# Exchanging kept exponentials through a DRAM buffer instead of by moves within SBUF, in a fused attention kernel

## The chip, the cores and the metric

One core of a Trainium2 chip runs the whole program. The metric is device time in microseconds (us): the median of several executions. The kernel was already tuned; it keeps TensorE, VectorE (DVE) and ScalarE (ACT) almost always at work, with GpSimd (POOL) and SyncE (SP) beside them for small sums and transfers.

## What is computed

`x` is 8 x 512 x 512 (batch, positions, features) in float32, with 16 heads of 32 features:

```python
Q = _split_heads(x @ Wq.T + bq);  K = _split_heads(x @ Wk.T + bk);  V = _split_heads(x @ Wv.T + bv)
cQ = Q + _split_heads(tokens @ Wq.T + bq)
cK = K + _split_heads(tokens @ Wk.T + bk)
scores = jnp.einsum('bhqd,bhkd->bhqk', cQ, cK) / jnp.sqrt(jnp.float32(HEAD_DIM))
attn = jax.nn.softmax(scores, axis=-1)
out = jnp.einsum('bhqk,bhkd->bhqd', attn, V)
# the result: x + out, heads joined again
```

## The kernel before

The work is cut into T = 32 steps: one step `t` is four heads of one of the eight batches. Steps 1 to 28 run in a software pipeline (`thirds`), each in three parts. In step t the kernel makes the row maxima of the scores of step t+1 (and begins those of t+2), the exponentials of t and t+1, the product of the exponentials with V for step t-1 (`weighted`), and a third of the projections of the next batch by seven-product block multiplication (`one_item`, `products`, `combine_x`).

The maxima need scores with queries on partitions; the product with V needs exponentials with keys on partitions. For half of the queries ScalarE computes the exponentials twice, once with queries on partitions for the sums and once with keys on partitions (L798). For the other half (query blocks 0 and 1 of the steps in `KEPT`, 1 to 29) it computes them once, with queries on partitions (`denominators`, L700), and **kept** in SBUF in `store`: `kept[t]` is 128 partitions x 4 blocks x 4 KB. They must then be transposed. VectorE does that within 32 x 32 blocks (`turn_kept`, L659), four instructions a step. What remains is to exchange blocks between the four groups of 32 partitions: block g of partition group a must trade places with block a of group g. There are six such pairs of 128 KB each.

Before, `swap_kept` makes this exchange with three DMAs for each pair: move 0 copies the one block aside (`between`, two spare slots of `store`), move 1 copies the other into its place, move 2 brings the first back from aside. Moves 0 and 1 for step t+1 stand at the end of step t, move 2 in the middle part of step t+1. SP issues some and POOL the others:

```python
later = 6 if t % 4 == 1 else 2
here = move == 2 or move == 0 and n >= later
(nc.gpsimd if here else nc.sync).dma_start(to, of)
```

`kept[t]` is read by TensorE in the next step, in the second half of the 32 products of `weighted` (`times_v_half`, L839).

The instructions of TensorE, ScalarE, VectorE and POOL stand in the order in which the program is written (`manual_schedule`); SP's are placed by a scheduler. Each engine works strictly in its own order and waits on semaphores.

POOL's other work in a step, in order: weighting and residual of the result (`send`, L912 and L913, which wait for VectorE's transpose L911), corrections to the projections (L538 to L540 for q, L532 for k, L1249, L1250 and L1238 for v), the split of the maxima into three bfloat16 parts (`split_max`, L714 to L717), the masked sums (`masked`, L864) and the bias (L203). In one step of four, sums of blocks of x are added (`combine_x`, L387 to L391). SP also issues the loads of x (`load_block`, L172), of the residual (`load_residual`, L190), the transposing DMA of the maxima (`turn_max`, L726) and the stores of the result (L916).

Of the kernel before, what the change touches and what calls it, by code (L numbers as in the profile page):

```python
# [9 lines left out]
F32 = mybir.dt.float32  # L10
# [7 lines left out]
def kernel(  # L18
# [38 lines left out]
    nc = tc.nc  # L57
    P = 128
    B, S, D = x.shape
# [3 lines left out]
    HG = P // HD  # L63
    NP = HG // 2
# [6 lines left out]
    KEPT = range(1, T - 2)  # L71
# [6 lines left out]
    op = ctx.enter_context(tc.tile_pool(name="op", bufs=2))  # L78
    ring = ctx.enter_context(tc.tile_pool(name="ring", bufs=1, space=bass.MemoryType.PSUM))

    psum = ring.tile([P, 8, 512], F32, tag="psum", name="psum")


# [47 lines left out]
    def begin(*ws):  # L131
        for w in ws:
            rows = order[w : w + 4]
            pairs = [(j, j + 1) for j in rows if j + 1 in rows]
            last = max(
                pairs, key=lambda p: rows.index(p[0]) + rows.index(p[1]), default=sorted(rows[2:])
            )
            order[w : w + 4] = [j for j in rows if j not in last] + list(last)
        row_of[0] = list(order)

    def released(*roles):
        order[:] = [row_of[0][i] for i in roles]
# [16 lines left out]
    BL = 32  # L159
    NB = S // BL  # L160

    def spread(a, d):

        return a.rearrange("(f j) d -> j f d", j=BL)[:, :, d : d + BL]

    def load_block(n):

        b, cc = divmod(n, NC)
        if b < B:
            xs[n] = xp.tile([P, NB, BL], F32, tag="x", name=f"x_{n}")  # L170
            for h in range(HG):
                nc.sync.dma_start(xs[n][h * BL : (h + 1) * BL], spread(x[b], cc * P + h * BL))  # L172
# [4 lines left out]
    def turned_by_vector(t):  # L177

        return t < T - 1

    def load_residual(t):

        b, g = divmod(t, G)
        if turned_by_vector(t):
            if t == T - 2:
                xr[t] = late[0][:, 2, :].rearrange("p (f e) -> p f e", e=BL)
            else:
                xr[t] = op.tile([P, NB, BL], F32, tag="xr", name=f"xr_{t}")
# [17 lines left out]
    store = EB.tile([P, 18, 2, S], F32, tag="eb", name="store")  # L206
# [20 lines left out]
    def load_w(n, w, queue, cs=range(NC)):  # L227
        wv = w.rearrange("(c p) d -> p c d", p=P)
        for c in cs:
# [7 lines left out]
                mybir.EngineType.Activation,  # L237
                mybir.EngineType.DVE,
                mybir.EngineType.Pool,
            }  # L240
        )
    )
# [133 lines left out]
    def load_blocks(most=B * NC):  # L376
        for _ in range(min(most, len(to_load))):
            load_block(to_load.pop(0))
# [185 lines left out]
    aside = const.tile([P, 2, 2, HS], F32, tag="aside", name="aside")  # L564
# [61 lines left out]
    def row_max_aside(t, qc):  # L626

        open_max(t)
        for j in range(HG):
            row_scores(t, qc, j, banks(j))  # L630
        nc.scalar.copy(spare, banks(0).rearrange("p (c f) -> p c f", f=P))  # L631
        for j in (1, 2, 3):
            one_max(t, qc, j, banks(j))

    def max_aside(t, qc):
        nc.vector.tensor_reduce(nmax[t][:, qc, 0:1, 0], spare, AX.XY, ALU.max, negate=True)
# [16 lines left out]
    kept = {}  # L653
# [4 lines left out]
        e = kept[t][:, :, n // NP, pr, :].rearrange("p g h s -> p g (h s)")  # L658
        nc.vector.transpose(e, e)  # L659

    APART = [(a, g) for a in range(HG) for g in range(a + 1, HG)]
    between = store[:, 16:18]

    def swap_kept(t, move, some=range(6)):

        later = 6 if t % 4 == 1 else 2

        def part(a, g):
            return kept[t][a * BL : (a + 1) * BL, g].rearrange("p c h s -> p (c h s)")

        for n in some:
            a, g = APART[n]
            at = (n + 2) % HG * BL
            aside = (store[:, 6:8] if t == KEPT[-1] else between)[at : at + BL, n // HG]
            aside = aside.rearrange("p i s -> p (i s)")
            to, of = [(aside, part(a, g)), (part(a, g), part(g, a)), (part(g, a), aside)][move]
            if t < KEPT[-1]:
                here = move == 2 or move == 0 and n >= later
            else:
                here = move > 0 and n >= 3  # L680
            (nc.gpsimd if here else nc.sync).dma_start(to, of)  # L681

    def denominators(t, qc, w=HG, js=range(HG)):

# [242 lines left out]
    part = {}  # L927
# [174 lines left out]
    turn_kept(1, 3)  # L1102
    combine_x(1, 1, nc.gpsimd)
    aparts[0] = masked(0)
    for move in range(2):
        swap_kept(1, move)

    MADE = [
        (n, u, product)
# [34 lines left out]
    def turn_more(t, i, after):  # L1144

        for _ in range((TURNED if t + 1 < KEPT[-1] else TURNED_LAST).get((i, after), 0)):
            if t + 1 in KEPT:
                n = turned[t + 1] = turned.get(t + 1, -1) + 1
                turn_kept(t + 1, n)
        even = t % 2 == 0  # L1150
        if (i, after) == ((2, 1) if even else (0, 2)) or (t, i, after) == (2, 0, 2):
            turn_x(next_x[0])
            next_x[0] += 1

    def thirds(t, made):

        b, r = divmod(t, G)
        of = (t - 1) // G + 1
        begin(0, HG)
        turn_more(t, 0, 0)  # L1160
        row_max_aside(t + 1, 1)
        max_aside(t + 1, 1)
        row_max(t + 1, 2, False, HG)
        turn_more(t, 0, 1)
        denominators(t + 1, 1, None, (1, 2, 3, 0))
        denominators(t + 1, 2, HG)
        weighted(t - 1, banks(0), banks(1), nothing)
        turn_more(t, 0, 2)
        load_blocks(1)
        one_item(of, *next(made), (2, 3), ignore, nothing)  # L1170
        released(0, 1, 4, 5, 7, 6, 2, 3)
        for i in (1, 2):
            begin(HG)
            rows = (t + 1, 3) if i == 1 else (t + 2, 0)
            if i == 1:
                joined(t, i - 1, rows)
                turn_more(t, i, 0)
                row_max(*rows, False, HG, False)
            else:
                exponentials_of_rest(t, i - 1)  # L1180
                turn_more(t, i, 0)
                row_max(*rows, False, HG)
            turn_more(t, i, 1)
            if i == 1:
                first = range(6 if t + 1 < KEPT[-1] else 3)
                swap_kept(t, 2, first)
                split_max(t + 1)
                turn_max(t + 1)
                swap_kept(t, 2, range(len(first), 6))
            dens = lambda js=range(HG): denominators(*rows, HG, js)  # L1190
            n, u, kind = next(made)
            if kind == "first":
                products(of, n, u, kind, False, dens, nothing, None)
                turn_more(t, i, 2)
            elif n == "v":
                small = nothing
                if t + 1 not in KEPT:
                    small = lambda: transpose_max(t + 1, banks(2), nc.scalar.copy)
                other_shared(of, n, u, dens, (0, 3), small, lambda: turn_more(t, i, 2))
                released(1, 2, 4, 5, 6, 7, 0, 3)  # L1200
            else:
                products(of, n, u, kind, False, dens, nothing, False)
                turn_more(t, i, 2)
            if i == 1:
                aparts[t] = masked(t)
            if (t + 1, i) == (KEPT[-1], 1):
                swap_kept(t + 1, 0)
            if i == 2:
                if r == 0:
                    combine_x(b + 1, 1, nc.gpsimd)  # L1210
                load_residual(t + 1)
            else:
                if t > 1:
                    bias_residual(t)
                if r == 0:
                    combine_x(b + 1, 0, nc.gpsimd)
            if i == 2 and t + 1 < KEPT[-1]:
                for move in range(2):
                    swap_kept(t + 1, move)

    def other_shared(b, n, u, dens, at, small, more):

# [44 lines left out]
    for t in KEPT[:-1]:  # L1267
        thirds(t, iter(MADE[(t - 1) % G * 3 :]))
# [56 lines left out]
    t = T - 3  # L1325
    begin(0, HG)
    first, second = row_of[0][:HG], row_of[0][HG:]
# [10 lines left out]
        row_max_of(t + 1, 2, 1, banks(HG + 2, 2))  # L1338
    row_max_of(t + 1, 2, 0, late[0][:, :2, :])
    bias_residual(t)  # L1340
    swap_kept(t, 1)
    apart = masked(t - 1)
    aparts[t] = masked(t)
    load_residual(t + 2)
    bias_residual(t + 2)
    swap_kept(t, 2)
    load_residual(t + 1)
    halves_of(t - 1, banks(0), (1,))
    row_of[0] = [*second[:2], *first[2:], *first]
# [22 lines left out]
    t = T - 2  # L1372
# [25 lines left out]
    t = T - 1  # L1398
# [48 lines left out]
    b, g = divmod(t, G)  # L1447
# [52 lines left out]
```

## Time and profile before

| | |
|---|---|
| median of 3 runs | 650.57 us (649.7 to 651.48) |
| the profiled execution | 650.74 us, span 648.9 us |
| granted TensorE clock | 1.0 throughout |
| busy share | PE 99%, DVE 93%, ACT 82%, POOL 63% |
| DMA | 102.01 MB, of them HBM read 19.75 MB and written 8.39 MB |
| exchange of kept exponentials | 264 DMAs on SP, 258 on POOL, 128 KB each |

PE is TensorE's matmuls, PEld its weight loads; q0 is the queue that POOL issues on, q1 SP's. A row of a timeline gives start, duration, engine, source line, operation, output and input, and in brackets the idle time before it with what ended it. L12 is line 12 of the kernel before; the changed kernel's lines stand one to four further down in most places.

### The profile page before, as it was taken

What the parts mean: (1) busy time and instruction counts of PE and PEld (TensorE: products, weight loads), DVE (VectorE), ACT (ScalarE), POOL (GpSimd) and SP (SyncE); (2) the same over time, 40 slices, a digit from 0 to 9 for tenths busy, and PEclk for the clock granted to TensorE, in tenths of its full rate; (3) what the DMA queues carried; (4) which work ended last, traced back from release to release, by engine and by line L of the source; (5) the groups of instructions that cost most, each with busy time, mean ns of one, the idle gap of its engine ahead of it and who ended that gap; (6) DMA issues with size and microseconds to landing.
All of it is one profiled execution on the core that took longest, in us unless ns stands there. A gap on an engine that the chain in (4) does not pass through costs nothing. (4 is left out here: it accounts for less than half of the span.)

```text
span 648.9 us, 24878 instructions
## 1 busy us (share of the span) xinstructions
PE 642.6 (99%) x9856; PEld 358.5 (55%) x9856; DVE 600.7 (93%) x845; ACT 533.6 (82%) x1364; POOL 409.6 (63%) x651
## 2 busy tenths in 40 slices
PE   9999999999999999999999999999999999999997
PEld 8445555556555555555555555555655555555541
DVE  3799999999999999999999999999999999999887
ACT  2479888889888889888888988898988888888564
POOL 3642555767666785668566585766767677675650
PEclk9999999999999999999999999999999999999999
DMA  7634588788779788878788887897877777777821
GB/s 187 106 48 68 121 183 175 158 180 178 155 172 181 156 190 181 190 155 172 173 184 172 171 170 152 177 198 158 180 152 180 176 162 153 165 177 161 201 37 33
DMA packets 248456, 102.01 MB, mean 157 GB/s; under 512 B 229962, under 2 KB 230474, under 8 KB 248340
## 3 DMA queue, kind: packets, MB, share of 16 engines
q1 hardware_dynamic: 234196, 65.54, 53.3%
q0 software_dynamic: 12384, 33.83, 19.2%
q8 instruction: 78, 1.28, 0.8%
q10 hardware_dynamic: 1760, 1.05, 0.6%
q14 instruction: 38, 0.31, 0.2%
HBM read 19.75 MB, written 8.39 MB: 43 GB/s over the span
## 5 line engine op out<-in xcount | busy, mean ns | idle before, releaser
L592 DVE TENSOR_REDUCE nmax<-psum 128x1 f32<-128x512 f32 x279 | 177.8, 676 | 9.9 <-PE psum L640 5.1
L681 POOL DMA_DIRECT2D store<-store x258 | 128.9, 502 | 77.3 <-DMA store<-store 51.9
L700 ACT ACTIVATE psum<-psum,nmax 128x512 f32<-128x512 f32 x248 | 165.1, 678 | 3.6 <-DVE nmax L592 3.0
L640 PE MATMUL psum<-kT,qT 32*128 32x512 f32 x1024 | 161.8, 612 | 0.0
L700 ACT ACTIVATE store<-psum,nmax 128x512 f32<-128x512 f32 x204 | 139.5, 700 | 24.7 <-DVE nmax L592 24.5
L798 ACT ACTIVATE store<-psum 128x512 f32<-128x512 f32 x232 | 119.8, 603 | 33.4 <-PE psum L784 33.4
L659 DVE STREAM_TRANSPOSE store<-store 128x1024 f32<-128x1024 f32 x116 | 138.9, 1217 | 0.0
L649 DVE TENSOR_REDUCE nmax<-psum 128x2 f32<-128x1024 f32 x98 | 118.9, 1213 | 0.0
L839 PE MATMUL psum<-store,v 128*32 128x256 f32 x1856 | 107.1, 381 | 0.6 <-issue 0.6
L839 PEld LDWEIGHTS psum<-store,v 128*32 128x32 f32 x1856 | 57.2, 110 | 57.9 <-ACT wT_q L631 21.2
L784 PE MATMUL psum<-qT,kT 32*128 32x256 f32 x928 | 83.8, 373 | 0.0
L640 PEld LDWEIGHTS psum<-kT,qT 32*128 32x128 f32 x1024 | 61.3, 183 | 35.5 <-issue 17.8
L912 POOL TENSOR_TENSOR res<-res,recs 128x512 f32<-128x512 f32 x30 | 31.4, 1045 | 75.4 <-DVE res L911 75.4
L784 PEld LDWEIGHTS psum<-qT,kT 32*128 32x128 f32 x928 | 60.8, 184 | 5.7 <-issue 0.3
L700 ACT ACTIVATION_READ_ACCUMULATOR psum<-psum,nmax 128x1 f32 x248 | 55.1, 222 | 0.0
L461 PE MATMUL psum<-wc_v,xc 128*32 128x256 f32 x768 | 47.7, 379 | 0.0
L203 POOL TENSOR_TENSOR xr<-xr,bvs 128x512 f32<-128x512 f32 x30 | 38.3, 1276 | 11.1 <-DMA x<-in_x_dram 11.1
L461 PE MATMUL psum<-xc,wc_q 128*32 128x256 f32 x720 | 44.8, 379 | 0.0
L461 PE MATMUL psum<-xc,wc_k 128*32 128x256 f32 x720 | 44.5, 379 | 0.0
L700 ACT ACTIVATION_READ_ACCUMULATOR store<-psum,nmax 128x1 f32 x204 | 44.4, 218 | 0.0
L913 POOL TENSOR_TENSOR res<-res,xr 128x512 f32<-128x512 f32 x30 | 38.3, 1276 | 2.4
L461 PE MATMUL psum<-xT,wT_k 128*32 128x256 f32 x480 | 34.5, 382 | 0.0
(191 smaller groups left out, 975.4 us busy)
## 6 DMA issues: line engine op xcount, KB each, us to landing
store<-store SPq DMA_DIRECT2D x264, 128.0 KB, 2.9
store<-store POOLq DMA_DIRECT2D x258, 128.0 KB, 3.8
out_dram<-res SPq DMA_DIRECT2D x122, 64.0 KB, 3.7
xr<-in_x_dram SPq DMA_DIRECT2D x120, 64.0 KB, 3.4
x<-in_x_dram SPq DMA_DIRECT2D x112, 64.0 KB, 3.5
w_q<-in_L_cond_Wq_dram SPq DMA_DIRECT2D x4, 256.0 KB, 4.5
w_v<-in_L_cond_Wv_dram SPq DMA_DIRECT2D x16, 64.0 KB, 2.5
w_k<-in_L_cond_Wk_dram SPq DMA_DIRECT2D x16, 48.0 KB, 2.8
```

Source lines behind the costliest of these rows:

```text
L203: nc.gpsimd.tensor_tensor(xr[t], xr[t], bias, ALU.add)
L461: nc.tensor.matmul(pt[r], still[:, r], moving, start=(kc == kcs[0]), stop=(kc == kcs[-1]))
L592: nc.vector.tensor_reduce(nmax[t][:, qc, j : j + 1, 0], pt, AX.X, ALU.max, negate=True)
L640: nc.tensor.matmul(pt, qkT["q", t][r, qc * P : (qc + 1) * P], qkT["k", t][r, :], start=True, stop=True,)
L649: nc.vector.tensor_reduce(nmax[t][:, qc, pr * 2 : pr * 2 + 2, 0], pt, AX.X, ALU.max, negate=True)
L659: nc.vector.transpose(e, e)
L681: (nc.gpsimd if here else nc.sync).dma_start(to, of)
L700: nc.scalar.activation(to, of, AF.Exp, bias=nmax[t][:, qc, j, :], accum_out=sums[t][:, qc, j, :],)
L784: nc.tensor.matmul(banks(j)[:, i * HS : (i + 1) * HS], qkT["k", t][r, kc * P : (kc + 1) * P], qkT["q", t][r, KQ * P :], start=False, stop= ...
L798: nc.scalar.activation(e[:, j], banks(j), AF.Exp)
L839: nc.tensor.matmul(pt[j * HD : (j + 1) * HD, half * HS : (half + 1) * HS], vs[b % 2][:, kc, (g * HG + j) * HD : (g * HG + j + 1) * HD], e, ...
L913: nc.gpsimd.tensor_tensor(y, y, xr.pop(t), ALU.add)
```

## The change

The exchange goes through a buffer in DRAM. `write_kept(t)` copies all twelve blocks that don't lie on the diagonal out of SBUF with six DMAs (one for each run of neighbouring blocks of a partition group); `read_kept(t)` brings them back, each to its new partition group, with six more. POOL issues all of them. The writes stand where moves 0 and 1 stood, the reads stand after the first third of the projections in the first part of the step, which is earlier than move 2 stood. SP's instructions are now in written order too, and the loads of x and of the residual are written behind the writes at the end of a step.

```diff
+    outside = ctx.enter_context(
+        tc.tile_pool(name="outside", bufs=2, space=bass.MemoryType.DRAM)
+    )
...
                 mybir.EngineType.Pool,
+                mybir.EngineType.SP,
...
-    APART = [(a, g) for a in range(HG) for g in range(a + 1, HG)]
-    between = store[:, 16:18]
-
-    def swap_kept(t, move, some=range(6)):
...
+    OTHERS = [(0, 1, 4), (1, 0, 1), (1, 2, 4), (2, 0, 2), (2, 3, 4), (3, 0, 3)]
+
+    def write_kept(t):
+
+        outer[t] = outside.tile([HG, BL, HG, NP * 2 * S // 2], F32, tag="kept", name=f"outer_{t}")
+        of = kept[t].rearrange("p g c h s -> p g (c h s)")
+        for a, lo, hi in OTHERS:
+            nc.gpsimd.dma_start(outer[t][a, :, lo:hi], of[a * BL : (a + 1) * BL, lo:hi])
+
+    def read_kept(t):
+
+        to = kept[t].rearrange("p g c h s -> p g (c h s)")
+        for g, lo, hi in OTHERS:
+            nc.gpsimd.dma_start(
+                to[g * BL : (g + 1) * BL, lo:hi],
+                outer[t][lo:hi, :, g].rearrange("a j f -> j a f"),
+            )
...
         turn_more(t, 0, 2)
-        load_blocks(1)
         one_item(of, *next(made), (2, 3), ignore, nothing)
         released(0, 1, 4, 5, 7, 6, 2, 3)
+        read_kept(t)
...
             if i == 1:
-                first = range(6 if t + 1 < KEPT[-1] else 3)
-                swap_kept(t, 2, first)
                 split_max(t + 1)
                 turn_max(t + 1)
-                swap_kept(t, 2, range(len(first), 6))
...
             if (t + 1, i) == (KEPT[-1], 1):
-                swap_kept(t + 1, 0)
+                write_kept(t + 1)
             if i == 2:
                 if r == 0:
                     combine_x(b + 1, 1, nc.gpsimd)
-                load_residual(t + 1)
+                if t + 1 == KEPT[-1]:
+                    load_blocks(1)
+                    load_residual(t + 1)
...
             if i == 2 and t + 1 < KEPT[-1]:
-                for move in range(2):
-                    swap_kept(t + 1, move)
+                write_kept(t + 1)
+                load_blocks()
+                load_residual(t + 1)
...
     bias_residual(t)
-    swap_kept(t, 1)
+    read_kept(t)
     apart = masked(t - 1)
     aparts[t] = masked(t)
     load_residual(t + 2)
     bias_residual(t + 2)
-    swap_kept(t, 2)
     load_residual(t + 1)
```

The order of TensorE, VectorE and ScalarE is the same line for line. The listing of POOL shows the change at two places. The first is the step after the blocks of x are combined, from the last sum of x (`xc`) over the result (`res`) and the corrections to q (`qT`). Before:

```order
L390 TENSOR_TENSOR xc<-xT 128x512
L391 TENSOR_TENSOR xc<-xT,xc 128x512
L912 TENSOR_TENSOR res_1937<-res_1937,recs_1935 128x512
L913 TENSOR_TENSOR res_1937<-res_1937,xr_1590 128x512
L538 TENSOR_TENSOR qT_1953<-qT_1953 128x256
L539 TENSOR_TENSOR qT_1953<-qT_1953 128x256
L540 TENSOR_TENSOR qT_1953<-qT_1953 128x256
L681 DMA store<-store 32x1024 x6
```

And now, where `outer` is the buffer in DRAM:

```order
L395 TENSOR_TENSOR xc<-xT,xc 128x512
L673 DMA outer_1840<-store 32x3072
L673 DMA outer_1840<-store 32x1024
L673 DMA outer_1840<-store 32x2048 x2
L673 DMA outer_1840<-store 32x1024
L673 DMA outer_1840<-store 32x3072
L913 TENSOR_TENSOR res_1919<-res_1919,recs_1917 128x512
L914 TENSOR_TENSOR res_1919<-res_1919,xr_1589 128x512
L542 TENSOR_TENSOR qT_1930<-qT_1930 128x256
L543 TENSOR_TENSOR qT_1930<-qT_1930 128x256
L544 TENSOR_TENSOR qT_1930<-qT_1930 128x256
```

Six writes now stand between the sum of x and the result; before, SP issued moves 0 and 1 of this step alone.

The second place is SP in the same and the next step: the transposed maxima (`maxT`), the residual (`xr`), the blocks of x, the moves and the results (`out_dram`). Before:

```order
L726 DMA_TRANSPOSE maxT_1746<-split 128x4x128
L190 DMA xr_1858<-in_x_dram 32x16x32
L172 DMA x_1948<-in_x_dram 32x16x32 x3
L681 DMA store<-store 32x1024 x12
L916 DMA out_dram<-res_1937 32x16x32 x4
L172 DMA x_1948<-in_x_dram 32x16x32
```

And now:

```order
L727 DMA_TRANSPOSE maxT_1728<-split 128x4x128
L175 DMA x_1847<-in_x_dram 32x16x32 x4
L193 DMA xr_1852<-in_x_dram 32x16x32 x4
L917 DMA out_dram<-res_1919 32x16x32 x4
L727 DMA_TRANSPOSE maxT_1998<-split 128x4x128
```

The moves are gone from SP, and the eight loads of a step stand together between the transposed maxima and the results.

More of the change, by code (lines that the diff above doesn't have):

```diff
@@ L659, in turn_kept @@
         nc.vector.transpose(e, e)
-    APART = [(a, g) for a in range(HG) for g in range(a + 1, HG)]
-    between = store[:, 16:18]
-    def swap_kept(t, move, some=range(6)):
[L666 to L681, printed above, removed]
+    outer = {}
+    OTHERS = [(0, 1, 4), (1, 0, 1), (1, 2, 4), (2, 0, 2), (2, 3, 4), (3, 0, 3)]
[11 more added lines that the diff above has]
+            )
     def denominators(t, qc, w=HG, js=range(HG)):
@@ L1104 @@
     aparts[0] = masked(0)
-    for move in range(2):
-        swap_kept(1, move)
+    write_kept(1)
     MADE = [
@@ L1217, in thirds @@
             if i == 2 and t + 1 < KEPT[-1]:
-                for move in range(2):
-                    swap_kept(t + 1, move)
+                write_kept(t + 1)
+                load_blocks()
+                load_residual(t + 1)
     def other_shared(b, n, u, dens, at, small, more):
```

## The prediction

> **What bounds the kernel now.** I read the page first, then the waits, then the timeline of each engine over four neighbouring steps. The page says who is busy:
>
> ```profile
> span 648.9 us, 24878 instructions
> PE 642.6 (99%) x9856; PEld 358.5 (55%) x9856; DVE 600.7 (93%) x845; ACT 533.6 (82%) x1364; POOL 409.6 (63%) x651
> q1 hardware_dynamic: 234196, 65.54, 53.3%
> q0 software_dynamic: 12384, 33.83, 19.2%
> ```
>
> TensorE, VectorE and ScalarE carry the span; GpSimd (POOL) is idle for a third of it, and the DMA queues are busy for some 73%. The list of waits says who waits for whom (total us, times, longest):
>
> ```profile
> POOL res L912 <- DVE res L911: 75.4, 27, 5.9
> POOL store L681 <- DMA store<-store: 51.9, 48, 3.2
> PEld psum L461 <- ACT store L798: 28.7, 50, 0.8
> PEld psum L839 <- ACT wT_q L631: 21.2, 28, 0.8
> DVE nmax L592 <- PE psum L640: 5.1, 11, 2.2
> PEld psum L461 <- POOL qT L538: 1.5, 4, 0.4
> PEld L771 <- DMA store<-store: 2.5, 6, 0.4
> ```
>
> TensorE waits for ScalarE, and VectorE for TensorE. The long waits on an exchange (L681) are POOL's own. Only 4 us of TensorE's waits are put down to POOL or a DMA, in pieces of at most 0.4 us. The query for the transpose that ends each step (L911) shows how regular this is:
>
> ```profile
> L911 DVE STREAM_TRANSPOSE res<-psum x28: 651/654/717, 73.6 to 591.5; 128x512 f32<-128x512 f32 x28
> ```
>
> 27 intervals in 517.9 us are 19.18 us a step. A step is therefore a ring of TensorE, ScalarE and VectorE, with POOL and the DMAs beside it. The listings of the two kernels show the same order on these three engines, line for line. So the change can gain nothing that these engines don't wait for today; it can only use up slack.
>
> **Part 1: POOL's time for the issues.** Per step 18 moves of 128 KB (9 of them on POOL on average) become 12 DMAs, all on POOL, and 24 blocks of 128 KB instead of 18. The only price in the trace is the move of 32 rows of 4 KB:
>
> ```profile
> L681 POOL DMA_DIRECT2D store<-store x258: 489/489/674, 78.9 to 613.8; - x129
> DMA to landing us min/median/max: 2.1/3.5/5.9
> ```
>
> A write names one run per partition (32 rows of 4, 8 or 12 KB), as the move does, so I take 0.49 us: 2.9 us for six. A read names one to three runs, 64 on average. If cost goes by the DMA it is 0.49 us, if it goes by the run 0.98 us, so six cost 2.9 to 5.9 us. I take 4.0, nearer to the lower end, since a part of the 0.49 must be fixed. The Trainium skill (DMA: Bandwidth & Descriptors, Anatomy of one DMA) says many descriptors can be emitted before their added cost shows; by that the six would cost 2.9. No run here shows it yet, as every move has the same 32 rows.
>
> What POOL has free in a step follows from two answers over four steps, first for L681 alone, then for all its work:
>
> ```profile
> sum 76.70, POOL 17.96; mean POOL 4.49
> sum 76.70, PE 76.70 PEld 43.55 DVE 73.77 ACT 67.21 POOL 52.92; mean PE 19.17 PEld 10.89 DVE 18.44 ACT 16.80 POOL 13.23
> ```
>
> Without the moves POOL works 34.96 us in 76.7. With 48 DMAs at 2.9 + 4.0 us a step it works 62.6; at 0.98 us each it would work 82.0, more than there is.
>
> **Part 2: POOL's order, where its results are needed.** The tightest place is the step after the blocks of x are combined (L391); there POOL runs without a gap. The timeline of POOL, then of VectorE:
>
> ```profile
> 294.79 0.27 POOL L714 CAST split<-nmax 128x16 bf16<-128x16 f32 x1
> ...
> 302.51 1.29 POOL L391 TENSOR_TENSOR xc<-xT,xc 128x512 f32<-128x512 f32 x1
> 304.06 1.05 POOL L912 TENSOR_TENSOR res<-res,recs 128x512 f32<-128x512 f32 x1 [0.26 <-DVE res L911]
> ...
> 307.24 0.73 POOL L539 TENSOR_TENSOR qT<-qT 128x256 f32<-128x256 f32 x1
> 307.92 0.74 POOL L540 TENSOR_TENSOR qT<-qT 128x256 f32<-128x256 f32 x1
> ...
> 318.02 2.00 POOL L681 DMA_DIRECT2D store<-store  x4 [0.20 <-issue]
> 323.24 1.04 POOL L912 TENSOR_TENSOR res<-res,recs 128x512 f32<-128x512 f32 x1 [3.22 <-DVE res L911]
> ...
> 326.40 0.73 POOL L1250 TENSOR_TENSOR v<-v 128x256 f32<-128x256 f32 x1
> ...
> 332.74 0.49 POOL L681 DMA_DIRECT2D store<-store  x1 [1.08 <-DMA store<-store]
> ```
> ```profile
> 309.42 0.42 DVE L554 TENSOR_TENSOR qT<-psum,qT 128x256 f32<-128x256 f32 x1 [0.24 <-ACT psum L700]
> 309.76 0.74 DVE L486 SCALAR_TENSOR_TENSOR qT<-psum,tok,qT 128x512 f32<-128x512 f32 x1
> ```
>
> Now POOL issues nothing between L391 and L912 (SP makes the moves there); afterwards the six writes stand between them (the listing with the diff). So 2.9 us of issuing move ahead of sums that VectorE needs. What comes before them moves too: the reads of the step before start when L1250 is done. That is 327.13 in the step of the same kind, so 38.4 us (two steps) sooner 288.7; with 0.5 us of waiting (part 3) and 4.0 of issuing they end at 293.2, where now L714 starts at 294.79. The 9.01 us of work up to the end of L391 (303.80) then end at 302.2, the writes at 305.1, and 3.91 us later (304.06 to 307.97) L539 at 309.0. VectorE uses that at 309.76: 0.8 us of slack are left, the wait is nil. With reads at 0.98 us it is 310.9 (1.1 us late), with all twelve so 313.9 (4.1 us). The place comes six times. In the other steps the 3.22 us before L912 cover the added 0.9 us of writes.
>
> **Part 3: data in time.** Every read waits for all six writes, so POOL stands still at the first one, and behind it stand the split of the maxima and the sums for L390. Then TensorE's second half of `weighted` waits for all six reads. The writes may start at 318.02 as L681 does now and are issued by 321.0. 12 blocks are 1.57 MB; q0 moved 33.83 MB in 19.2% of 648.9 us, 271 GB/s, so 5.8 us: 324.3 if they flow from 318.5. From the end of the flow to the semaphore I add 3.3 us (3.8 from issue to landing less 0.5):
>
> ```profile
> store<-store POOLq DMA_DIRECT2D x258, 128.0 KB, 3.8
> store<-store SPq DMA_DIRECT2D x264, 128.0 KB, 2.9
> out_dram<-res SPq DMA_DIRECT2D x122, 64.0 KB, 3.7
> xr<-in_x_dram SPq DMA_DIRECT2D x120, 64.0 KB, 3.4
> x<-in_x_dram SPq DMA_DIRECT2D x112, 64.0 KB, 3.5
> ```
>
> 327.6: POOL, free at 327.13, waits 0.5 us. The reads are issued by 331.6 (now the last move is at 332.74), their data flow until 333.9 and have landed at 337.2.
>
> ```profile
> 336.85 3.18 PEld L839 LDWEIGHTS psum<-store,v 128*32 128x32 f32 x64 [0.76 <-ACT wT_q L631]
> ```
>
> The second half begins at 338.4, so 1.2 us are left. The bounds: loads of x and of the residual share the engines (SP will issue eight in a row, behind the transposed maxima). q1's 53.3% are 346 us; less SP's 264 moves at q0's rate (128 us) they leave 218 us for 354 transfers of 64 KB, the weights and the transposed maxima, by estimate 0.5 us for a load, so eight could add 4 us. Then the writes land at 331.6, the reads at 341.2, 2.8 us late. Below, with no queueing, the slack is 2 us or more.
>
> SP loses its nine moves and its order is now fixed: outputs, transposed maxima, x, residual. x and the residual are loaded a step ahead of use, and the maxima are used in the next step; so I cost it at nothing, and the cover is most of a step of 19.18 us. The start keeps its order on the three engines: nothing. At the end the last exchange has less room:
>
> ```profile
> 599.00 2.36 DVE L659 STREAM_TRANSPOSE store<-store 128x1024 f32<-128x1024 f32 x2
> ```
> ```profile
> 619.06 1.45 PEld L839 LDWEIGHTS psum<-store,v 128*32 128x32 f32 x32 [0.76 <-ACT store L1318]
> ```
>
> Its writes can start at 601.4; by the same durations (0.5 + 5.8 + 3.3 for them, 9.6 for the reads) they have landed at 611.0 and the reads at 620.6, 1.5 us after TensorE wants them. With little else on the queues there it may be nothing; I take 0.5.
>
> **The sum.** The profiled run took 650.74 us for a span of 648.9 (1.84 us around it); the median of three is 650.57. Steps 0, start 0, end 0.5: 651.2.
>
> **The rivals.** (a) POOL's sums come late after L391: 1.1 to 4.1 us six times, 7 to 25 us, 658 to 676. It decides once a read costs over 0.8 us. For it: POOL has no gap there now. Against: the slack above. (b) The reads land late and TensorE waits for a DMA in each of 28 steps: 0.5 to 2.8 us, 14 to 78 us, 665 to 729, likelier in the lower half. It decides once write and read together take 1.2 us longer than in part 3. For it: the DMA engines now go from 18 to 24 blocks, and DRAM writes land later for their size (64 KB in 3.7 us against 128 KB in 2.9). The Trainium skill (the same section) says the semaphore waits for the write's receipt and that HBM's is the heaviest; the trace agrees in its sign, with 0.8 us. Against: today three moves in a row fit into the same stretch. (c) POOL becomes the bound at 82.0 us in four steps: 5.3/4 us, 28 times, 37 us, 688. (d) Faster: fewer bytes cross SBUF per exchange (24 block accesses for 36), and VectorE's transposes of `store` or ScalarE's exponentials shorten; 0.1 us a step would be 2.8 us, 648. Nothing in the waits speaks for it.
>
> **How the numbers follow.** No change 0.37, (a) 0.17, (b) 0.28, (c) 0.10, (d) 0.08. A change of 0.3% (2 us) is about what a measurement of this kernel can tell. Slower is (a) + (b) + (c), 0.55; same 0.37; faster 0.08. The forecast's own range is 649.5 to 652.5; the range reaches from (d)'s 648.5 to 690, leaving out the upper part of (b), some 0.15, and a little below.
>
> **What would show it.** Right: L911's successor 19.18 us apart, POOL waiting under 2 us at the first read, no wait of TensorE or VectorE for POOL or a DMA over 1 us. (a) shows as waits of L558/L490 for POOL every fourth step, (b) as TensorE at L840 waiting for a DMA in each step, (c) as POOL busy over 95%, (d) as shorter instructions. A read above 0.8 us or writes that need over 10 us to land make the forecast wrong.

## The result and the profile after

The changed kernel takes 693.34 us (median), the kernel before, on the same chip, 651.03 us: a ratio of 1.064, 95% interval 1.0601 to 1.0679. One of its four runs was in a slower state (702.44 us, at a granted clock of 0.975), as was one of the four with two queues below (694.89 us); the medians count them, the ratios leave them out. The profiled execution took 694.2 us for a span of 692.4 us. It is slower, by 43.5 us of span, and 3 us beyond the upper end of the range. The page:

```profile
span 692.4 us, 24189 instructions
PE 652.0 (94%) x9856; PEld 365.0 (53%) x9856; DVE 605.0 (87%) x845; ACT 536.6 (77%) x1364; POOL 461.2 (67%) x741
q0 software_dynamic: 22272, 91.25, 52.3%
q1 hardware_dynamic: 221524, 30.92, 36.4%
```

TensorE runs the same 9856 matmuls as before and stands still for 6% of the span; they take 652.0 us for 642.6, and its clock is halved in four stretches before its last matmul (last section). The waits of the same kernel say what it stands still for. In the lines of the changed kernel L840 is the product with V (L839 before), L673 the writes, L679 the reads, L206 the bias on the residual (L203 before):

```profile
PEld psum L840 <- issue: 41.1, 43, 6.8
PE psum L840 <- DMA store<-outer: 27.6, 15, 6.0
POOL store L679 <- DMA outer<-store: 16.9, 12, 2.5
POOL xr L206 <- DMA xr<-in_x_dram: 11.6, 4, 6.8
```

The first two rows are one wait, seen at the weight loads and at the matmuls: the second half of `weighted` waits for the reads. No wait of VectorE for POOL is in the list. The transpose that ends each step, L912 now, gives the length of a step, and the line of the reads what an issue costs:

```profile
L912 DVE STREAM_TRANSPOSE res<-psum x28: 652/655/718, 73.5 to 621.0; 128x512 f32<-128x512 f32 x28
```
```profile
L679 POOL DMA_DIRECT2D store<-outer x174: 502/534/619, 78.9 to 648.2; - x174
```

(621.0 - 73.5)/27 is 20.28 us a step, for 19.18. So the 43.5 us lie in three places: 29.6 us in 27 steps; 9.2 us in the two intervals behind them, up to the last result transposes (27.82 and 11.61 us for 26.41 and 3.82); and 4.9 us behind the last of these (32.0 us for 27.2). The start is as long as before.

What a long step looks like, on POOL first, where the blocks of x are combined (L391 to L395):

```profile
300.05 3.20 POOL L679 DMA_DIRECT2D store<-outer  x6 [0.83 <-DMA outer<-store]
...
309.89 1.28 POOL L394 TENSOR_TENSOR xc<-xT 128x512 f32<-128x512 f32 x1
311.12 1.28 POOL L395 TENSOR_TENSOR xc<-xT,xc 128x512 f32<-128x512 f32 x1
312.35 2.98 POOL L673 DMA_DIRECT2D outer<-store  x6
...
322.35 2.68 POOL L679 DMA_DIRECT2D store<-outer  x5 [2.40 <-DMA outer<-store]
```

and then on TensorE's weight loads, two steps of the same kernel:

```profile
309.63 1.45 PEld L840 LDWEIGHTS psum<-store,v 128*32 128x32 f32 x32 [0.76 <-ACT wT_q L635]
311.24 1.57 PEld L840 LDWEIGHTS psum<-store,v 128*32 128x32 f32 x32 [0.15 <-issue]
...
328.80 1.45 PEld L840 LDWEIGHTS psum<-store,v 128*32 128x32 f32 x32 [0.76 <-ACT wT_q L635]
332.79 1.48 PEld L840 LDWEIGHTS psum<-store,v 128*32 128x32 f32 x32 [2.54 <-issue]
```

In the first of the two steps the halves follow each other, as before. In the second the first half ends at 330.25, and the other half begins 2.54 us later: the last read lands at 332.47. From the first write (312.35) to the first read is 10.0 us, from there to the end of the wait (332.79) 10.44 us, in all 20.4 us. The writes had been held behind L394 and L395.

### The profile page after: what moved, and what is told of

Its sections match the earlier page's. It is cut to its first block, busy times and chain, and to the rows that moved or that the text cites. A ratio compares the mean times of both kernels' runs of the same rounds, so it can differ in the third digit from the quotient of the medians.

```text
span 692.4 us, 24189 instructions
## 1 busy us (share of the span) xinstructions
PE 652.0 (94%) x9856; PEld 365.0 (53%) x9856; DVE 605.0 (87%) x845; ACT 536.6 (77%) x1364; POOL 461.2 (67%) x741
## 3 DMA queue, kind: packets, MB, share of 16 engines
q0 software_dynamic: 22272, 91.25, 52.3%
q1 hardware_dynamic: 221524, 30.92, 36.4%
## 4 chain that ended last, share of the span: by engine, by line
PE 38%; DMA 29%; POOL 18%; DVE 5%; issue 5%; ACT 1%; SPq 1%; POOLq 0%; DVEq 0%
PE psum L465 19%; DMA store<-outer 14%; DMA outer<-store 11%; POOL store L679 5%; PE psum L644 5%; PE psum L840 5%; POOL outer L673 4%; PE psum L785 3%; PE psum L408 2%; DMA xr<-in_x_dram 2%; POOL v L1238 2%; DMA out_dram<-res 1%; POOL res L914 1%; PE psum L772 1%; POOL res L913 1%
## 5 line engine op out<-in xcount | busy, mean ns | idle before, releaser
L840 PE MATMUL psum<-store,v 128*32 128x256 f32 x1856 | 115.9, 396 | 27.8 <-DMA store<-outer 27.6
L679 POOL DMA_DIRECT2D store<-outer x174 | 93.0, 541 | 23.5 <-DMA outer<-store 16.9
L840 PEld LDWEIGHTS psum<-store,v 128*32 128x32 f32 x1856 | 60.4, 113 | 90.1 <-issue 41.1
L673 POOL DMA_DIRECT2D outer<-store x174 | 86.7, 505 | 8.9 <-DVE store L663 6.5
L206 POOL TENSOR_TENSOR xr<-xr,bvs 128x512 f32<-128x512 f32 x30 | 38.4, 1280 | 24.8 <-DMA x<-in_x_dram 13.2
```

The source lines that it names most:

```text
L673: nc.gpsimd.dma_start(outer[t][a, :, lo:hi], of[a * BL : (a + 1) * BL, lo:hi])
L679: nc.gpsimd.dma_start(to[g * BL : (g + 1) * BL, lo:hi], outer[t][lo:hi, :, g].rearrange("a j f -> j a f"),)
L840: nc.tensor.matmul(pt[j * HD : (j + 1) * HD, half * HS : (half + 1) * HS], vs[b % 2][:, kc, (g * HG + j) * HD : (g * HG + j + 1) * HD], e, ...
```

## The experiments

A step here is the mean over 27 intervals of the transpose, the end the two intervals behind them, the rest what follows up to the end of the span, all from the trace of each kernel. Ratios are to the kernel before in the same session (649.88 to 651.03 us), with their 95% intervals.

| kernel | us | ratio | step | end | rest |
|---|---|---|---|---|---|
| before | 650.57 | 1 | 19.18 | 26.4, 3.8 | 27.2 |
| changed | 693.34 | 1.064 (1.0601 to 1.0679) | 20.28 | 27.8, 11.6 | 32.0 |
| half rows | 654.05 | 1.0066 (1.0042 to 1.0090) | 19.14 | 26.4, 3.8 | 31.9 |
| three quarters | 656.06 | 1.0079 (1.0048 to 1.0110) | 19.18 | 27.6, 4.0 | 32.0 |
| wide writes | 679.93 | 1.0455 (1.0393 to 1.0518) | 19.93 | 27.9, 11.6 | 28.1 |
| long runs | 689.01 | 1.0614 (1.0576 to 1.0653) | 20.04 | 26.9, 10.3 | 32.0 |
| last exchange half | 686.86 | 1.0548 (1.0499 to 1.0597) | 20.18 | 28.9, 3.8 | 32.0 |
| early half | 676.78 | 1.0404 (1.0345 to 1.0462) | 20.03 | 27.9, 10.7 | 27.2 |
| two queues | 689.76 | 1.0589 (1.0530 to 1.0647) | 20.58 | 27.4, 6.2 | 28.0 |
| half rows in SBUF | 661.12 | 1.0172 (1.0149 to 1.0195) | 19.49 | 26.4, 5.1 | 28.7 |
| half rows, more DMAs | 649.99 | 0.9999 (0.9984 to 1.0014) | 19.17 | 26.4, 3.8 | 27.1 |
| old moves, SP written | 664.11 | 1.0214 (1.0183 to 1.0244) | 19.67 | 27.5, 5.4 | 27.1 |
| exchange only | 747.02 | 1.1456 (1.1411 to 1.1501) | 22.40 | 35.4, 3.8 | 31.9 |
| writes first | 677.22 | 1.0393 (1.0354 to 1.0432) | 19.64 | 27.8, 11.5 | 33.2 |
| all three | 667.60 | 1.0252 (1.0224 to 1.0280) | 19.57 | 33.5, 3.9 | 27.6 |

### Is it the data of the exchange? Half of each row, and three quarters

```diff
-  nc.gpsimd.dma_start(outer[t][a, :, lo:hi], of[a * BL : (a + 1) * BL, lo:hi])
+  nc.gpsimd.dma_start(outer[t][a, :, lo:hi, :512], of[a * BL : (a + 1) * BL, lo:hi, :512])
```

The reads likewise; with 768 for 512 it is three quarters. All twelve issues, their places and waits stay.

> Only the first half (2 KB) of every exchanged row is written and read back; the other half stays where it was, so the data of half a block is not exchanged. The twelve DMAs, their order and their waits are as in the changed kernel. Theory T (the DMA engines are full: 24 blocks of 128 KB and the small loads take more engine time than a step has room for) expects 650 to 656 us, since half the bytes are gone. Theory L (a fixed chain of write, receipt, wait on GpSimd, read is too long, whatever the bytes) expects 675 us or more. Theory S (the new written order of SyncE, with eight loads in one burst, is what delays things) expects 680 us or more.

> The changed kernel, but only the first 3 KB of each exchanged row of 4 KB are moved. Theory T (there is a deadline some 20 us after the first write, and only what lands behind it costs): the reads end 17 to 18 us after the first write, no step is longer than 19.3 us, 652 to 658 us, as with half the bytes. Rival C (each byte slows the engines or the queues, without a deadline): halfway between half and whole, steps of 19.6 to 19.8 us, 670 to 676 us.

Both came out as theory T has it: with half rows every step is as before, with three quarters every step but one (19.90 us; the kernel before has one of 19.85). The transposes with half rows, and the weight loads with three quarters, which follow each other in the step that was 2.54 us late:

```profile
L912 DVE STREAM_TRANSPOSE res<-psum x28: 650/653/657, 73.1 to 590.0; 128x512 f32<-128x512 f32 x28
```
```profile
336.66 3.18 PEld L840 LDWEIGHTS psum<-store,v 128*32 128x32 f32 x64 [0.76 <-ACT wT_q L635]
```

So there is a deadline, and bytes that land ahead of it cost nothing: neither POOL's added issues nor the traffic as such lengthens a step. From the records of the single packets, medians over the steps, in us from the first write's issue:

| of each row | write's data end | first read | reads' data take | reads' data end |
|---|---|---|---|---|
| 2 KB | 5.92 | 9.75 | 5.59 | 15.30 |
| 3 KB | 7.65 | 9.75 | 7.55 | 17.25 |
| 4 KB | 8.98 | 10.01 | 10.12 | 20.16 |

The second 0.79 MB costs the write 3.06 us (257 GB/s) and the reads 4.53 us (174 GB/s). With whole rows 20.16 us is longer than a step of the ring: 17 of 28 times the next writes are issued before the reads' data have ended, with half rows once. The time of half rows fell only to 1.0066 all the same: the last stretch stays 4.9 us longer (below).

### Is it the place of the writes on POOL?

```diff
             if i == 2:
+                if t + 1 < KEPT[-1]:
+                    write_kept(t + 1)
                 if r == 0:
                     combine_x(b + 1, 1, nc.gpsimd)
...
             if i == 2 and t + 1 < KEPT[-1]:
-                write_kept(t + 1)
                 load_blocks()
```

> The changed kernel with one move in GpSimd's order: in the step in which the blocks of x are combined, the six writes stand ahead of the second half of that combination (2.5 us of POOL's work) instead of behind it. Theory T (the deadline of the reads is missed by 2 to 3 us in that step because its writes are issued later than in the others): its writes start 2.5 us sooner in the step, its second half of weighted stops waiting, and these steps (20.6 to 24.1 us) fall to 19.9 to 20.4 us: 12 to 18 us less in all, 674 to 682 us. Rival (the long steps come from the combination and the sums behind it, not from the data): the steps stay, 690 to 695 us.

677.22 us, 16 us less: theory T again. The longest step is 20.40 us for 24.07. POOL, and TensorE's weight loads, in the step of the same kind as the one above:

```profile
305.65 2.99 POOL L673 DMA_DIRECT2D outer<-store  x6
308.66 1.29 POOL L394 TENSOR_TENSOR xc<-xT 128x512 f32<-128x512 f32 x1
...
315.94 3.20 POOL L679 DMA_DIRECT2D store<-outer  x6 [0.21 <-issue]
```
```profile
324.50 1.45 PEld L840 LDWEIGHTS psum<-store,v 128*32 128x32 f32 x32 [0.76 <-ACT wT_q L635]
326.89 1.48 PEld L840 LDWEIGHTS psum<-store,v 128*32 128x32 f32 x32 [0.94 <-issue]
```

The wait is 0.94 us for 2.54. So of the 29.6 us in the steps, 17 come from the writes held behind 2.5 us of sums in one step of four. The other 12.5 are smaller misses of the same deadline, in steps of every kind: with the writes first TensorE's second half still waits 0.5 to 2.2 us in 15 of 27 steps, mostly in every second one.

### Which part of the flow is slow?

> The six writes of 32 partitions become four writes of all 128 partitions, 4 KB runs, which also copy the diagonal blocks: 2.10 MB instead of 1.57 MB a step. The reads stay six of 32 partitions. If T holds because only 32 partitions are read at a time (the write phase took 8.4 to 9.4 us for 1.57 MB), the writes should end 2 us or more sooner in spite of their bytes, and the time falls to 655 to 680 us. If T holds by bytes alone, a third more to write makes it 700 to 715 us. L expects 685 to 700 us, two issues fewer and no other difference.

> The changed kernel, but the loads of x and of the residual and the stores of the results of batches 0 to 6 move 32 rows of 2 KB in place of 512 runs of 128 bytes: same bytes, same DMAs, the data lands in another arrangement, so the result is not the reference's. T expects most of the 36% of engine time of the SyncE queue to go and the time to fall to 652 to 670 us. L expects 688 to 695 us. S expects a part of the loss to go, 670 to 690 us.

Long runs is this edit, for the loads of x, of the residual, and the stores but those of the last batch:

```diff
-  nc.sync.dma_start(xs[n][h * BL : (h + 1) * BL], spread(x[b], cc * P + h * BL))
+  nc.sync.dma_start(
+      xs[n][h * BL : (h + 1) * BL].rearrange("p f e -> p (f e)"),
+      x[b][cc * P + h * BL : cc * P + (h + 1) * BL, :],
+  )
```

Wide writes: four DMAs of 128 partitions, the diagonal blocks with them, for six of 32.

```diff
-  for a, lo, hi in OTHERS:
-      nc.gpsimd.dma_start(outer[t][a, :, lo:hi], of[a * BL : (a + 1) * BL, lo:hi])
+  for g in range(HG):
+      nc.gpsimd.dma_start(outer[t][g].rearrange("a j f -> (a j) f"), of[:, g])
```

They move a third more bytes in the same time (2.10 MB, data end at 8.88 us; 236 GB/s over the phase for 175), and the reads' data end at 19.43 us for 20.16. The time lies at the end of the first expected range, but not for its reason, since the writes end no sooner; 4 of the 13 us saved are in the last stretch (28.1 us for 32.0, below). Long runs: the loads of x and the residual and most stores of results move 2 KB runs for 128 byte runs (the numbers in them are then not the kernel's). q1's share of the DMA engines fell from 36.4% to 25.2%, the exchange's data ended hardly sooner (8.82 and 19.43 us), and the kernel is barely faster. The loads' small packets are not what makes the exchange late.

> The changed kernel, but half of the six writes and half of the six reads (those of the partition groups 2 and 3) are issued by SP, in its written order ahead of the loads. All bytes move. Theory P (what limits a write or read is that one queue works on 32 partitions at a time: four wide writes moved 2.10 MB in the time of 1.57 MB): two groups are under way at once, the writes' data take 5 to 7 us instead of 9 and the reads' too, steps of 19.2 us, 652 to 660 us with the end shorter as well. Theory M (the rate of DRAM or of the DMA engines limits): 9 us each as before, steps of 20 us and more, 685 us and above. POOL then has 174 DMAs instead of 348.

```diff
-  nc.gpsimd.dma_start(outer[t][a, :, lo:hi], of[a * BL : (a + 1) * BL, lo:hi])
+  queue = nc.gpsimd if a < 2 else nc.sync
+  queue.dma_start(outer[t][a, :, lo:hi], of[a * BL : (a + 1) * BL, lo:hi])
```

The reads likewise. 689.76 us, against theory P. SP's reads are mostly issued 1 to 8 us behind POOL's, because SP has the eight loads and the stores in front of them, so the run is no clean test of the time. But where packets of both queues flow at once (297 to 302 us), their sum is 207 to 308 KB in a us by the records of packets, and one queue alone reaches 289 (POOL's, at 338 us) and 374 (SP's, at 317). The residual comes late as well:

```profile
POOL xr L206 <- DMA xr<-in_x_dram: 47.0, 12, 5.8
PE psum L842 <- DMA store<-outer: 25.3, 11, 4.3
```

> The changed kernel with the exchange split by time: whole blocks of 128 partitions are written (four writes for six, a third more bytes), the first 2 KB of each row two thirds into the step, as soon as they are turned, the second 2 KB at its end. All bytes move. Theory T: at the end of the step only half of the write's data stand ahead of the reads, so these end 15 to 17 us after that write instead of 19.7, before the deadline: steps of 19.2 to 19.4 us; the end stays long (27.8 and 11.6 us), 662 to 670 us. Rival D (the DMA engines as a whole are full, not the place of the data): steps of 19.9 us or more, 680 us and above. Rival P (the two more issues a step make POOL late): steps of four kinds, every fourth one over 21 us, 675 us and above.

```diff
-  if (t + 1, i) == (KEPT[-1], 1):
-      write_kept(t + 1)
+  if i == 1 and t + 1 <= KEPT[-1]:
+      write_kept(t + 1, (0,) if t + 1 < KEPT[-1] else (0, 1))
...
-  write_kept(t + 1)
+  write_kept(t + 1, (1,))
```

Here the second argument names the halves of each row that are written, as four wide writes each. 676.78 us: by its steps of 20.03 us rival D, though 3 us below the range that D gave; a quarter of the steps over 21 us, as rival P has it, is not seen (one is). q0 has packets under way for 85% of the time from 150 to 550 us, for 76% in the changed kernel, and its share of the DMA engines rose to 58.0%. How much of this is the third more bytes the run doesn't show.

> Half rows, with the buffer in SBUF instead of DRAM (six writes, and twelve reads of 32 rows of 2 KB, since a read of several groups can't be one DMA there; 522 DMAs on POOL). Theory M (DRAM is what makes the flow slow): the write's data end 4 to 5 us after the first issue for 5.9, the packets are shorter. Theory P (the 32 partitions make it slow, DRAM costs nothing much): 5.5 to 6.5 us for the write. POOL issues 3 us more a step; in time 650 to 660 us by both, or 675 to 690 us if POOL becomes late every fourth step.

```diff
-  outer[t] = outside.tile([HG, BL, HG, NP * 2 * S // 2], F32, tag="kept", name=f"outer_{t}")
+  outer[t] = store[:, 16:18].rearrange("p c i s -> p (c i) s")
```

The write's data end at 6.57 us for 5.92, so for the writes DRAM as such isn't what is slow. This run shows something else: with 18 DMAs a step on POOL six steps, those with the combination, take 20.7 to 20.9 us, and VectorE waits for POOL's sums there, which it does in no step of the changed kernel:

```profile
DVE qT L558 <- POOL qT L543: 6.9, 4, 1.9
```

That is rival (a), at 1.5 us in one step of four for six more issues.

### SP's order

> The kernel before, with its moves within SBUF, but SyncE in written order and the loads of x and of the residual behind the moves at the end of the step, as the change has them. T and L expect 650 to 654 us: this part of the change costs nothing. S expects over 670 us.

> The changed kernel with SP's part undone: SP's order is again the scheduler's and the loads of x and the residual are asked for where they were before; only the exchange through DRAM stays. Theory T (the data of write and read need more time than the step leaves): the steps stay at 20.0 to 20.4 us and the end at 27.8 and 11.6 us, in all 685 to 696 us. Theory S (the written order of SP and its eight loads in a row cost some 14 us, as they did with the old moves): 673 to 683 us, with steps of 19.6 to 19.9 us.

Two halves of the change, each alone. The first takes these lines into the kernel before, the second takes them out of the changed one:

```diff
                 mybir.EngineType.Pool,
+                mybir.EngineType.SP,
...
-        load_blocks(1)
         one_item(of, *next(made), (2, 3), ignore, nothing)
...
             if i == 2 and t + 1 < KEPT[-1]:
...
+                load_blocks()
+                load_residual(t + 1)
```

The first, with the old moves, costs 14 us, half of it in a single step of 26.74 us: the written order puts SP's moves ahead of the loads, and by the list of waits POOL waits for the residual. The second costs 97 us, far outside both expectations. Their waits, first the one and then the other:

```profile
POOL xr L203 <- DMA xr<-in_x_dram: 84.5, 25, 5.7
```
```profile
PEld L771 <- DMA maxT<-split: 46.8, 11, 6.3
PE psum L771 <- DMA maxT<-split: 41.5, 11, 5.8
```

In the exchange alone TensorE waits for the transposed maxima, which happens once in the changed kernel, for 0.5 us; its waits before the product with V are no longer than there (38.2 us at the weight loads, for 41.1). SP's timeline of it shows them behind the loads, and four loads take up to 7.6 us to issue here (0.58 us each by median in the kernel before):

```profile
394.26 3.52 SPq L916 DMA_DIRECT2D out_dram<-res  x4
397.82 7.62 SPq L193 DMA_DIRECT2D xr<-in_x_dram  x4
405.57 4.27 SPq L726 DMA_TRANSPOSE maxT<-split  x1
```

In the changed kernel the maxima stand ahead of the loads. So SP's part of the change saves 54 us in it (747.02 less 693.34). Order and place of the loads were changed together; which of the two does it isn't shown.

### The end

> The changed kernel, but of the last exchange alone only the first 2 KB of each 4 KB row are moved; the other 28 stay whole. Theory T: the steps stay at about 20.3 us, and the two intervals at the end fall from 27.8 and 11.6 us to 26.4 and 3.8 us, so some 9 us sooner, with what follows up to 14: 678 to 685 us. Rival (the end is long because POOL and SP come to it late, not because of its own data): 27.8 and 11.6 us remain, 690 to 695 us.

```diff
+            w = 512 if t == KEPT[-1] else 1024
-            nc.gpsimd.dma_start(outer[t][a, :, lo:hi], of[a * BL : (a + 1) * BL, lo:hi])
+            nc.gpsimd.dma_start(outer[t][a, :, lo:hi, :w], of[a * BL : (a + 1) * BL, lo:hi, :w])
```

The second interval falls from 11.61 to 3.82 us, the first grows by 1.0, so that exchange costs some 7 us. As expected in kind; the total, 686.86, is 2 us above the expected range.

The 4.9 us in the last stretch are in kernels with 348 DMAs on POOL whatever they move. A DRAIN on POOL, at the end, lasts 2.70 us before (258 DMAs), 10.06 in the changed kernel (348), 5.33 with wide writes (290), 4.92 with the early half (406); the number behind the last slash is the longest of three. First before, then the changed kernel:

```profile
L1495 POOLq DRAIN  x3: 34/102/2702, 642.9 to 648.6; - x3
```
```profile
L1494 POOLq DRAIN  x3: 34/102/10057, 681.6 to 692.2; - x3
```

So half rows were tried again with 58 DMAs more:

```diff
+        for a in range(2):
+            nc.gpsimd.dma_start(outer[t][a, :1, a, 512:640], of[a * BL : a * BL + 1, a, 512:640])
```

> Half rows (2 KB of each 4 KB row are moved), and beside the six writes of each exchange two more of one row of 512 bytes to DRAM, which nobody reads: 406 DMAs on POOL instead of 348. With half rows alone the work ended before that of the kernel before and yet the time was 3.4 us longer, since GpSimd's drain at the end took 10.06 us for 2.70. Theory N (the drain depends on the number of DMAs issued by POOL, since it was 4.92 us in the kernel with 406): the drain takes about 4.9 us and the kernel 648 to 650 us, though more is issued. Rival (it depends on what is moved or on the buffer in DRAM): 10.06 us, 654 us or more.

649.99 us, no different from the kernel before (0.9984 to 1.0014), with more work than half rows alone:

```profile
L1496 POOLq DRAIN  x3: 34/102/4913, 641.8 to 647.5; - x3
```

As far as these runs show, the number of POOL's DMAs sets this drain, and not in proportion. What it counts was not found.

### All causes taken away

> All causes found, taken away at once, with all bytes moved: the writes ahead of the second half of the combination; four whole writes of 128 partitions for six of 32 (291 DMAs on POOL, for which GpSimd's last drain should take 5.4 us for 10.06); and of the last exchange the first 2 KB of each row written a third of a step sooner. Theory T: steps of 19.2 to 19.6 us, the end shorter by 3 to 6 us, 656 to 666 us, still not below the kernel before, since the ring sets 19.16 us. Rival (something not yet found costs a good part of the 43 us): 672 us or more.

Beside the edits of writes first and wide writes:

```diff
         read_kept(t)
+        if t + 1 == KEPT[-1]:
+            write_kept(t + 1, (0, 1))
...
             if (t + 1, i) == (KEPT[-1], 1):
-                write_kept(t + 1)
+                write_kept(t + 1, (1, 2))
```

Here the second argument is the range of halves of each row. 667.60 us, between the two expectations. Steps of 19.57 us and a rest of 27.6 us are as theory T has them. At the end the second interval is 3.87 us, but the first grew to 33.5 us: there TensorE now waits once for the transposed maxima:

```profile
623.10 0.11 PEld L775 LDWEIGHTS <-onesb 3*128 3x128 bf16 x4 [5.78 <-DMA maxT<-split]
```

The last exchange was made earlier at the price of SP's transfer beside it. It isn't back at 650 us: the steps still miss the deadline by 0.4 us on average, and the last 17 us lie there (10), at the end (7), and in the drain (0.5). No version faster than the kernel before was found; with the steps at 19.17 us (half rows) the ring sets the time, as in the kernel before.

## Why the prediction was wrong

**The ring** held: 19.14 to 19.18 us a step wherever the data are in time, though POOL issues all twelve DMAs.

**Part 1** held. A write costs 0.490 us, as taken, a read 0.534 us, so six cost 3.2 us where 4.0 were taken, and 5.9 were the bound. The sentence of the Trainium skill (DMA: Bandwidth & Descriptors, Anatomy of one DMA), by which many descriptors add little, agrees with that row: a read of three runs a row takes 0.544 or 0.613 us, one of a single run 0.502 or 0.517. Rival (c), POOL as the bound, fell: it is busy for 67%.

**Part 2** is the step that failed. It worked out that in the step with L391 the writes are issued from 302.2 to 305.1, and asked of this place only when L539's sum is done. That was right, no wait for it is seen. But part 3 took the flow of data for the ordinary step alone, with writes from 318.02. By the same durations the writes of 302.2 put the reads at 321.4, and TensorE wants them at 338.4 less a step of 19.17, 319.2: 2.2 us late, from the prediction's own numbers. The trace has 2.54 us at that place, and 1.91 to 3.87 us in the six steps of this kind. With the writes ahead of the second half of the combination 16 us of the 43 are gone.

**Part 3** had the mechanism and a size too small against the slack it left. Predicted were 9.6 and 9.6 us, measured 10.0 and 10.44 in the step shown. The writes' rate was nearly right (257 GB/s for 271), the reads' was not (174). From the first write to the landing of the last read the prediction reckoned 19.2 us, with 20.4 allowed (318.02 to 338.4). The median of the changed kernel is 21.1 us, with the writes first 20.9: 1.9 us more than predicted, for a slack of 1.2. So the ordinary steps miss the deadline a little too, and with the writes first all misses together cost 12.5 us. A landing time spreads; a slack smaller than the error of its terms should not have been counted as no wait. The bound on the loads (4 us) was no part of it, as long runs show.

The kernel before had missed the same deadline once. There its last move lands at 492.43, and the interval behind is the one of 19.85 us:

```profile
490.15 1.45 PEld L839 LDWEIGHTS psum<-store,v 128*32 128x32 f32 x32 [0.76 <-ACT wT_q L631]
492.70 1.48 PEld L839 LDWEIGHTS psum<-store,v 128*32 128x32 f32 x32 [1.09 <-issue]
```

The list of waits has it under "issue", so the reading that TensorE waits for a DMA only in pieces of 0.4 us passed it over.

**SP at nothing** was wrong in both signs: its order costs 14 us with the old moves and saves 54 us with the exchange. The cover named, a step of lead for the loads, is nearly true of the loads (within the steps POOL waits for the residual twice, 1 us each), but not of the transposed maxima that stand in the same queue: they land after 7.3 us now (2.7 before).

**The end** was taken at 0.5 us, with a bound of 1.5; the last exchange costs some 7 us. And the drain at the very end (4.9 us) was in no part of the sum, nor was the halved clock (last section; some 4 us in three steps). The end and the drain carry the result beyond the range.

**The rivals.** (b) is what happened, at 1.10 us a step on average, inside the 0.5 to 2.8 it gave, though TensorE waits 0.5 us or more in 16 of 27 steps and not in each; it had been given less than no change (0.28 for 0.37). (a) did not happen here, but six more DMAs a step bring it (half rows in SBUF). (d) has nothing: half rows with the drain paid back end at 649.99 us.

## What to carry to other kernels

Give each transfer that is waited for its deadline in every kind of step, and above all in the one where the issuing engine is fullest: a move of issues behind 2.5 us of sums cost more here than the longer way through DRAM did in all the other steps. A slack of a microsecond on a path of twenty, through DMA engines that are busy for 89% of the time (52.3% and 36.4%), is a wait. When an engine's queue carries both bulk loads and a small transfer that someone waits for, its order can be worth more than its bytes.

## What the runs showed of the hardware that was not expected

TensorE's clock is halved after a wait of some 3 us. In the step after 167 us the reads came 3.87 us late; the granted clock is 0.75 and 0.68 in the two stretches behind, and 32 weight loads then take from 171.77 to 174.56 us, 2.79 us for 1.48 us in a step with a wait of 2.54 us; their 32 matmuls take 3.44 us for 1.93:

```profile
170.00:173.00 3.00, 1.20 (x12) 0.68 (x16) 1.16 (x2) 2.65 (x8) 0.00 (x0) 0.75 0.92 192
173.00:176.00 3.00, 3.00 (x52) 1.74 (x47) 0.56 (x2) 0.00 (x0) 0.00 (x0) 0.68 1.05 408
```
```profile
171.77 0.23 PEld L840 LDWEIGHTS psum<-store,v 128*32 128x32 f32 x8 [3.87 <-issue]
...
174.33 0.23 PEld L840 LDWEIGHTS psum<-store,v 128*32 128x32 f32 x4 [0.20 <-issue]
```

The column before the last two is the granted clock. The same follows waits of 3.67 and 3.21 us, but not one of 3.12 us, behind which 32 weight loads take 1.48 us as ever:

```profile
415.10 1.48 PEld L840 LDWEIGHTS psum<-store,v 128*32 128x32 f32 x32 [3.12 <-issue]
...
578.24 0.23 PEld L840 LDWEIGHTS psum<-store,v 128*32 128x32 f32 x8 [3.21 <-issue]
```

So a DMA that is late by 3 to 4 us can cost 1.3 to 1.5 us more than its lateness, some 4 of the 17 us that the held writes cost.

Where the line lies can be worked out. In the changed kernel the half clock begins at 171.48, 495.75, 577.67 and 652.76 us, for 3.41 us each and 6.83 the last time; these times lie 95, 24 and 22 times 3.413 us apart, so there is a fixed grid. Before 578.24 TensorE neither loads weights nor multiplies for 2.73 us, of which 2.17 lie in one stretch of the grid; before 415.10 it is 2.64 us, but 1.37 and 1.27 in two. Over all 15 traces, a stretch at full clock with 2.1 us or more of such idle time is always followed by one at half clock, one with 2.0 us or less never. The Trainium skill (TensorE: Matmul & The Clock Gate, What's actually happening) gives half the clock after an idle window of about 3.4 us, the windows running freely; the grid agrees, but here a window need not be idle throughout: 2.1 us of 3.41 are enough.

Two queues did not flow faster than one (at most 308 KB in a us for 374), and wide writes did flow faster than narrow ones (236 for 175 GB/s). The Trainium skill (DMA: Bandwidth & Descriptors, Rules for kernel authors) says both: transfers to separate partitions share the same engines, and one of 128 partitions is to be preferred. The runs agree; why the narrow ones are slower they don't show.
